# Scaled V in three bfloat16 parts for the neighbour product, and moved turns and constants, in a four-layer graph network

## The chip, the cores and the metric

The kernel runs on one core of one Trainium2 chip. The metric is the device time of one execution in microseconds (us); lower is better. The core has a matrix engine (PE), a vector engine (DVE), a scalar engine (ACT), a general engine (POOL) and a queue for transfers (SP). Each engine works through its own queue strictly in order; semaphores make one wait for another.

## The reference

There are 512 nodes with 512 features and 16,384 edges (src, dst), and four residual blocks on x, each fed with h = max(layernorm(x), 0): a graph convolution, a four-layer sparse attention with a conditioned norm, a diffusion, and a two-layer relational network with gates. The change is mostly about the third block's adjacency, prepared early:

```python
adj = zeros(N, N); adj[row, col] = 1; adj[col, row] = 1; adj = adj + eye(N)
adj = adj / maximum(adj.sum(axis=1, keepdims=True), 1.0)
out = w[0] * h
cur = h
for i in range(3):
    cur = adj @ cur
    out = out + w[i + 1] * cur
return relu(out)
```

With A the symmetric 0/1 matrix plus identity and R the diagonal of inverse row sums, the three steps are R A, R A R A and R A R A R A. The kernel builds V = A R A and S = w1 A + w2 V + w3 A R V once, so that the whole diffusion later is one product with S, scaled by R.

## The kernel before

The node matrices lie as four chunks (K = 4) of 128 nodes by 512 features. The order of the work on every engine is that of the Python text: the kernel schedules by hand, and no planner moves anything. A product of a 128x128 block with 128x512 f32 values is one call in the text and two PE instructions of 0.43 us; a bfloat16 call is one instruction of 0.22 us. Two PSUM buffers ("ps") serve most products, four ("sp") others, two ("tr") the turns, which is what this text calls the transposes on PE with a copy out by ACT (`transposed`, L116 to L122).

The stages in order of time: the edges become one-hot matrices and window products that count edges and weights (to about 92 us); degrees and the two graph convolution layers (to about 140); the neighbour stage with the entry into attention (to 186); four attention layers, each with a multilayer perceptron (to about 650); diffusion (to 692); the two relational layers (to the end). All along, DVE mixes 60 basis matrices into the relational weights with 120 operations of 2.3 us (L216, L218), placed by calls of `more(n)`, which do n of them; POOL loads a basis of 1 MB whenever one of three buffers comes free.

Names that matter here, in the neighbour stage (L796 to L939):

- `enter_a` to `enter_d` take chunk c of x through the outer norm (relu of it by ACT, L816) and the inner, conditioned norm on DVE, which gives ys[c]. `norm_T(yT, ys[c], c)` turns ys[c] into yT, and `v_part(c)` multiplies it with wv.
- `v_rows(m)` computes the upper part of block row m of V from adj and three exact bfloat16 parts of R A (q_adj): row m is 512, 384, 256 or 128 columns wide. `mirrored` fills the lower part by turns.
- `radj` is A scaled by R in f32, made by four ACT operations (L885). `s_rows(m)` multiplies radj with V in f32, and `s_start` prepares the other terms of S in D1. S lies in the buffer of adj.
- `log_counts` and `log_end` prepare the logarithms of the edge counts for the attention scores.

In an attention layer the output projection follows the heads: `rows_of(c, heads)` adds the heads' products of chunk c, DVE adds them to z (L1086), `norm_chunk` makes ys[c], `norm_T` turns it, and `m1(half, j)` is the first matrix of the perceptron on half the nodes. One `more` call stands before the projection and one in the perceptron.

In the diffusion and the relational layers `plain_norm(c)` needs two ACT operations (Ln and Exp, L133 and L134), and `plain_T` turns its result.

At the start POOL builds the identity and the ids, issues its fifteen transfers of constants, and then computes `freq` (seven small operations and an iota) and fills `edge_of` and `sizes` (an iota and 36 fills), which are read from about 40 us on.

Of the kernel before, what the change touches and what calls it, by code (L numbers as in the profile page):

```python
# [9 lines left out]
F32 = mybir.dt.float32  # L10
F16 = mybir.dt.float16
BF16 = mybir.dt.bfloat16
I32 = mybir.dt.int32
AF = mybir.ActivationFunctionType
OP = mybir.AluOpType
# [4 lines left out]
P = 128  # L20
N = 512
D = 512
E = 16384
K = N // P
EC = E // P
H = 4
NB = 4
# [28 lines left out]
def row_bcast(v, parts=P):  # L56

    n = 1
    for s in v.shape:
        n *= s  # L60
    return bass.AP(tensor=v.tensor, offset=v.offset, ap=[[0, parts], [1, n]])
# [6 lines left out]
def network(ctx, tc, a, out, flag_i, general):  # L68
# [44 lines left out]
    def nodes(xT, c, w, **kw):  # L113

        return product([(xT[:, k, chunk(c)], w[:, k, :]) for k in range(K)], **kw)
# [113 lines left out]
    def more(n):  # L229
        for _ in range(n):  # L230
            next(terms, None)
# [20 lines left out]
    with ExitStack() as pe:  # L252
# [36 lines left out]
        sel = edges.tile([P, 32], F32, name="sel")  # L289
        nc.gpsimd.tensor_tensor(sel, ident[:, 0:32], ident[:, 32:64], op=OP.add)  # L290
        nc.gpsimd.tensor_tensor(sel, sel, ident[:, 64:96], op=OP.add)
        nc.gpsimd.dma_start(b_gcn, a["L0_gnn_b_gcn"].rearrange("l (k p) -> p l k", p=P))
        for l, r in enumerate((row1, row2)):
            nc.gpsimd.dma_start(r, row_bcast(a["L0_gnn_b_mlp"][l]))
        phase = edges.tile([64, N], F32, name="phase")
        nc.gpsimd.dma_start(phase, row_bcast(a["node_vec1"], 64))
        f_w1 = edges.tile([64, 16], F32, name="f_w1")
        nc.gpsimd.dma_start(f_w1, a["L1_gnn_f_w1"])
        f_w2 = edges.tile([16, 16], F32, name="f_w2")
        nc.gpsimd.dma_start(f_w2, a["L1_gnn_f_w2"])  # L300
        f_b = edges.tile([16, 2], F32, name="f_b")
        nc.gpsimd.dma_start(f_b[:, 0:1], a["L1_gnn_f_b1"].rearrange("(p o) -> p o", o=1))
        nc.gpsimd.dma_start(f_b[:, 1:2], a["L1_gnn_f_b2"].rearrange("(p o) -> p o", o=1))
        for t, n in ((bq, "bq"), (bk, "bk"), (bv, "bv"), (b1, "m_b1")):
            nc.gpsimd.dma_start(t, a["L1_gnn_" + n].rearrange("b (k p) -> p b k", p=P))
        nc.gpsimd.dma_start(dw, row_bcast(a["L2_gnn_diffusion_weights"]))
        nc.gpsimd.dma_start(att[:, 0, :], row_bcast(a["L3_gnn_att1"]))
        nc.gpsimd.dma_start(att[:, 1, :], row_bcast(a["L3_gnn_att2"]))

        freq = edges.tile([64, 4], F32, name="freq")  # L310
        nc.gpsimd.iota(freq[:, 0:1], pattern=[[0, 1]], base=0, channel_multiplier=1,
# [14 lines left out]
        for i, (lo, hi, _, c0, c1) in enumerate(PIECES):  # L326
            nc.gpsimd.memset(edge_of[:, 0, i : i + 1], float(c1))
            nc.gpsimd.memset(edge_of[:, 1, i : i + 1], float(c0))
            if i in (0, 2):
                nc.gpsimd.memset(sizes[:, :, i:], float(hi - lo))  # L330

        def look_for_stray():

# [461 lines left out]
    def norm_T(yT, y, c):  # L795
        transposed(yT[:, :, chunk(c)], [y[:, chunk(k)] for k in range(K)], nc.scalar.copy)  # L796
# [21 lines left out]
    def enter_c(c):  # L818
        mv = moments(z[:, c, :])
        inner[c] = rsqrt_start(mv[:, 1:2], EPS, [P, 1])  # L820
        ys[c] = att_y.tile([P, D], F32, name="y")
        nc.vector.scalar_tensor_tensor(ys[c], z[:, c, :], mv[:, 0:1], mod[:, 0, c, :], op0=OP.subtract, op1=OP.mult)

    def enter_d(c):
        n = rsqrt_end(*inner[c])
        nc.vector.scalar_tensor_tensor(ys[c], ys[c], n, mod[:, 1, c, :], op0=OP.mult, op1=OP.add)

    def v_part(c):
        if general:
            nc.vector.tensor_tensor(v[:, c, :], nodes(yT, c, wv), bv_row, op=OP.add)  # L830
        else:
            nc.scalar.copy(v[:, c, :], nodes(yT, c, wv))
# [3 lines left out]
    V = CP  # L836

    def upper(m, parts):
        ps = sp.tile([P, D], F32, name="sp")
        calls(ps[:, m * P :], [(lhs[:, k, chunk(m)], rhs[:, k, m * P :]) for k in range(K) for lhs, rhs in parts])  # L840
        return ps[:, m * P :]
# [4 lines left out]
    def s_start(m):  # L846
        d = D1[:, m, m * P :]
        nc.vector.tensor_scalar(d, d, dw[:, 1:2], None, op0=OP.mult)
        nc.vector.scalar_tensor_tensor(d, V[:, m, m * P :], dw[:, 2:3], d, op0=OP.mult, op1=OP.add)

    def s_rows(m):
        nc.vector.scalar_tensor_tensor(S[:, m, m * P :], upper(m, [(radj, V)]), dw[:, 3:4], D1[:, m, m * P :],
                                       op0=OP.mult, op1=OP.add)

    def mirrored(res, m):
        if m < K - 1:
            transposed(res[:, m + 1 :, chunk(m)], [res[:, m, chunk(q)] for q in range(m + 1, K)], nc.scalar.copy)

    def log_counts(k):

        nc.vector.tensor_scalar(lnC[:, k, :], C[:, k, :], 1.0, None, op0=OP.max)
        nc.scalar.activation(lnC[:, k, :], lnC[:, k, :], AF.Ln)
        nc.vector.tensor_scalar(C[:, k, :], C[:, k, :], 0.0, NEG, op0=OP.is_equal, op1=OP.mult)
# [17 lines left out]
    v_rows(1)  # L881
    enter_c(0)
    mirrored(V, 0)
    for k in range(K):
        nc.scalar.mul(radj[:, k, :], adj[:, k, :], rinv[:, k : k + 1])  # L885
    enter_c(1)
    enter_d(0)
    enter_a(3)
# [13 lines left out]
    enter_c(2)  # L902
    s_start(2)
    s_start(3)
    S = act.tile([P, K, N], F32, name="adj")
    s_rows(0)
    enter_d(2)
    v_part(1)
    enter_b(3)
    norm_T(yT, ys[2], 2)  # L910
    log_counts(1)
    s_rows(1)
    enter_c(3)
    mirrored(S, 0)
    log_counts(2)
    if not general:
        ps = mm.tile([P, N], F32, name="ps")
        for j in range(3):
            nc.tensor.matmul(ps[:1, :1], n_bad[:, j : j + 1], ones, start=(j == 0), stop=(j == 2))
        nc.vector.tensor_scalar(flag_i, ps[:1, :1], 0.5, None, op0=OP.is_gt)  # L920
    v_part(2)
    enter_d(3)
    s_rows(2)
    norm_T(yT, ys[3], 3)
    mirrored(S, 1)
    s_rows(3)
    log_end(0)
# [10 lines left out]
    with ExitStack() as ph:  # L938
# [61 lines left out]
        for i in range(NB):  # L1000
# [52 lines left out]
            def rows_of(c, heads, ps=None, last=False):  # L1053

                first = ps is None
                if first:
                    ps = mm.tile([P, D], F32, name="ps")
                calls(ps, [(oT[:, j, chunk(c)], wo[:, j, :]) for j in heads], first=first, last=last)
                return ps

            ps_ = [rows_of(0, (0, 1))]
            more(6)
            pT = att_p.tile([P, K, N], F32, name="pT", bufs=2)
            turn(pT, head, (0, 1))
            ps_.append(rows_of(1, (0, 1)))
# [11 lines left out]
            for c in range(K):  # L1077
                if c < 2:
                    ps = rows_of(c, (3, 2), ps_[c], last=True)
                else:  # L1080
                    ps = rows_of(c, (0, 1))
                    if c == 3:
                        norm_T(yT, ys[1], 1)
                        ys.append(norm_chunk(mod, 2))
                    rows_of(c, (2, 3), ps, last=True)
                nc.vector.tensor_tensor(z[:, c, :], ps, z[:, c, :], op=OP.add)  # L1086
                if c == 2:
                    norm_T(yT, ys[0], 0)
                else:
                    ys.append(norm_chunk(mod, c))  # L1090
            tT = one.tile([P, K, N], F32, name="oT")

            def m1(half, j):
                cols = slice(half * 256, half * 256 + 256)
                ps = mm.tile([P, D], F32, name="ps")
                for k in range(K):
                    nc.tensor.matmul(ps[:, :256], w1[:, k, chunk(j)], yT[:, k, cols],  # L1097
                                     start=(k == 0), stop=(k == K - 1))
                nc.scalar.activation(tT[:, j, cols], ps[:, :256], AF.Relu, bias=b1[:, i, j : j + 1])  # L1099

            m1(0, 0)
            norm_T(yT, ys[2], 2)
            m1(0, 1)
            m1(0, 2)
            norm_T(yT, ys[3], 3)
            m1(0, 3)
# [4 lines left out]
            else:  # L1111
# [3 lines left out]
                bo = load_row(a["L1_gnn_bo"][i + 1])  # L1115
                mod = new_mod()
                modulation(mod, 0)
            more(6 if i < NB - 1 else 5)
            for j in range(K):
                m1(1, j)  # L1120
            if i == NB - 1:
# [35 lines left out]
    def plain_norm(c):  # L1157

        y = late.tile([P, D], F32, name="y", bufs=4)
        mv, n = stats(x[:, c, :])  # L1160
        nc.vector.tensor_scalar(y, x[:, c, :], mv[:, 0:1], n, op0=OP.subtract, op1=OP.mult)
        return y

    def plain_T(hT, y, c, copy=relu_neg):
        transposed(hT[:, :, chunk(c)], [y[:, chunk(k)] for k in range(K)], copy)
# [2 lines left out]
    ys = []  # L1168
    for c in range(K):
        nc.vector.tensor_tensor(x[:, c, :], nodes(tT, c, w2), x[:, c, :], op=OP.add)  # L1170
        ys.append(plain_norm(c))
        if c == 2:
            plain_T(hT, ys[0], 0)
    plain_T(hT, ys[1], 1)
    cur = one.tile([P, 2, K, D], F32, name="mod")
    for c in range(K):
        nc.vector.tensor_tensor(cur[:, 0, c, :], nodes(hT, c, w_diff), b_diff, op=OP.add)
# [7 lines left out]
    for c in range(K):  # L1185
        tot = cur[:, 1, c, :]
        nc.vector.scalar_tensor_tensor(tot, nodes(S, c, cur[:, 0, :, :]), rinv[:, c : c + 1], tot,
                                       op0=OP.mult, op1=OP.add)
        nc.vector.scalar_tensor_tensor(x[:, c, :], tot, 0.0, x[:, c, :], op0=OP.max, op1=OP.add)
        ys.append(plain_norm(c))  # L1190
        if c == 2:
            plain_T(hT, ys[0], 0)


    wr = wl1
    for l in range(2):
# [29 lines left out]
            u2 = late.tile([P, R, K, D], BF16, name="u2")  # L1226
            u = [[u01[:, 0, r, :, :], u01[:, 1, r, :, :], u2[:, r, :, :]] for r in range(R)]
        ws = [w.rearrange("p (k o) -> p k o", k=K) for w in wr]
        plain_T(hT, ys[1], 1, turned)
        gates = [gates_start(0)]  # L1230
        for c in range(K):
            ps0, ps1 = (nodes(hT, c, ws[r], pool=sp, name="sp") for r in range(R))
# [87 lines left out]
```

## Time and profile before

| | |
|---|---|
| runs | 825.98, 826.07, 827.73 us; median 826.07 |
| profiled execution | 826.12 us, span 824.3 us |
| PE busy, 140 to 168 us | 26.30 of 28.00 us |
| PE busy, 168 to 186.24 us | 17.92 of 18.24 us; DVE 12.62, ACT 7.53 |
| PE busy, 262 to 385 us (one layer's length) | 122.45 of 123.00 us; DVE 114.42 |
| PE busy, 692 to 819.6 us | 126.80 of 127.60 us; DVE 78.47 |
| first window product on PE (L598) | starts at 9.31 us |
| first q projection of attention on PE | starts at 186.24 us |

A row of a timeline below gives start and length in us, the engine, the source line, the operation, out<-in with shapes, how many alike were merged, and in brackets the idle time before it with what ended it. The list of waits gives, for an engine and a releasing line, the total, the number and the longest.

### The profile page before, as it was taken

The numbers are of one execution on the slowest core, as the hardware profiler recorded it, in microseconds if no ns is written. First come the engines' busy times: TensorE is split into PE (matmuls) and PEld (weight loads), VectorE is DVE, ScalarE is ACT, GpSimd is POOL, SyncE is SP. The second block draws the span as 40 slices with busy tenths as digits, with TensorE's granted clock in tenths as the row PEclk, the third lists the DMA queues.
The fourth block names the chain that finished last, engine by engine and source line by source line (L and its number), as shares of the span: only waits on it lengthen the run. The fifth ranks groups of instructions, "written<-read, shape, count | busy, mean of one in ns | idle before, by whom it ended". The sixth has DMA issues, their size and how long they took to land.

```text
span 824.3 us, 8236 instructions
## 1 busy us (share of the span) xinstructions
PE 805.4 (98%) x2586; PEld 391.3 (47%) x2597; DVE 679.9 (82%) x1199; ACT 326.0 (40%) x657; POOL 64.3 (8%) x135
## 2 busy tenths in 40 slices
PE   7999999999999999999999999999999999999997
PEld 3444344454444744444644445644445644444445
DVE  5977986978889999889997889999889977789530
ACT  5454414534652424662424752324653122310410
POOL 8000010000000101001101000101010100000000
PEclk9999999999999999999999999999999999999999
DMA  9200155305658557587558586655599631122001
GB/s 231 74 7 17 43 215 193 114 2 167 182 164 286 180 184 230 139 247 268 184 162 285 148 259 226 200 161 190 146 297 384 214 92 53 47 84 100 1 13 41
DMA packets 50833, 128.38 MB, mean 156 GB/s; under 512 B 7008, under 2 KB 7808, under 8 KB 49760
## 3 DMA queue, kind: packets, MB, share of 16 engines
q0 software_dynamic: 17552, 66.83, 25.4%
q1 hardware_dynamic: 32944, 60.84, 23.8%
q8 instruction: 22, 0.36, 0.2%
q14 instruction: 27, 0.22, 0.1%
q10 hardware_dynamic: 288, 0.13, 0.1%
HBM read 108.90 MB, written 6.29 MB: 140 GB/s over the span
## 4 chain that ended last, share of the span: by engine, by line
PE 61%; issue 18%; DVE 13%; DMA 4%; ACT 2%; POOL 1%; SPq 0%; DVEq 0%; POOLq 0%
PE ps L101 31%; PE ps L1097 7%; PE sp L101 7%; DVE wrel L218 7%; PE win L598 4%; PE sp L968 4%; PE ps L376 4%; DMA basis<-in_L_gnn_basis_dram 2%; PE tr L121 2%; PE sp L702 1%; DVE st L158 1%; DMA w<-in_L_gnn_root_dram 1%; DMA w<-in_L_gnn_W_mlp_dram 1%; ACT p L974 1%; DVE y L792 1%
## 5 line engine op out<-in xcount | busy, mean ns | idle before, releaser
L218 DVE SCALAR_TENSOR_TENSOR wrel<-basis,att,wrel 128x2048 f32<-128x2048 f32 x116 | 264.8, 2342 | 1.4 <-DMA basis<-in_L_gnn_basis_dram 1.4
L101 PE MATMUL ps<-w,oT 128*128 128x512 f32 (+1 forms) x296 | 130.5, 584 | 1.3 <-DVE z L1086 1.3
L101 PE MATMUL ps<-yT,w 128*128 128x512 f32 x256 | 112.9, 594 | 0.0
L101 PE MATMUL ps<-w,yT 128*128 128x512 f32 x224 | 101.1, 595 | 1.2 <-ACT yT L128 0.7
L202 POOL DMA_DIRECT2D basis<-in_L_gnn_basis_dram x60 | 45.1, 752 | 674.4 <-DVE wrel L218 529.1
L101 PEld LDWEIGHTS ps<-w,oT 128*128 128x128 f32 x296 | 53.9, 190 | 62.7 <-issue 51.4
L101 PEld LDWEIGHTS ps<-yT,w 128*128 128x128 f32 x256 | 48.2, 190 | 61.9 <-issue 60.9
L101 PEld LDWEIGHTS ps<-w,yT 128*128 128x128 f32 x224 | 41.1, 190 | 47.2 <-issue 43.8
L133 ACT ACTIVATE g<-mv,eps_t 128x1 f32<-128x1 f32 (+1 forms) x45 | 13.3, 295 | 117.8 <-DVE mv L160 116.4
L1097 PE MATMUL ps<-yT,w 128*128 128x256 f32 x256 | 58.3, 381 | 0.0
L968 PE MATMUL sp<-kT,qT 128*128 128x512 f32 x128 | 57.5, 592 | 0.0
L972 DVE CUSTOM_DVE_ANT_0 ns<-sp,lnC 128x512 f32<-128x512 f32 x64 | 43.6, 689 | 13.7 <-PE sp L968 13.5
L974 ACT ACTIVATE p<-ns,stat 128x512 f32<-128x512 f32 x64 | 45.6, 713 | 22.9 <-DVE stat L972 22.5
L1097 PEld LDWEIGHTS ps<-yT,w 128*128 128x128 f32 x256 | 47.4, 190 | 10.6 <-ACT oT L1099 3.1
L598 PE MATMUL win<-s_hot,st 128*128 128x512 bf16 x189 | 50.5, 379 | 0.3
L579 DVE TENSOR_SCALAR s_hot<-node_ids,e_c 128x512 bf16<-128x512 f16 x128 | 39.4, 354 | 6.1 <-PE win L598 5.9
L960 ACT ACTIVATE p<-p,stat 128x512 f32<-128x512 f32 x64 | 43.7, 706 | 0.0
L968 PEld LDWEIGHTS sp<-kT,qT 128*128 128x128 f32 x128 | 24.3, 190 | 30.6 <-issue 30.1
L704 ACT ACTIVATE mod<-sp 128x512 f32<-128x512 f32 x64 | 32.9, 599 | 8.6 <-PE sp L702 8.6
L598 PEld LDWEIGHTS <-st 128*128 128x128 bf16 x195 | 18.5, 98 | 37.3 <-issue 24.3
L121 PEld LDWEIGHTS tr<-ident,y 128*128 128x128 f32 x176 | 21.5, 141 | 23.1 <-issue 16.3
L963 DVE STREAM_TRANSPOSE turned<-p 128x512 f32<-128x512 f32 x48 | 31.0, 685 | 1.7 <-issue 0.6
(276 smaller groups left out, 1076.9 us busy)
## 6 DMA issues: line engine op xcount, KB each, us to landing
basis<-in_L_gnn_basis_dram POOLq DMA_DIRECT2D x60, 1024.0 KB, 6.7
pT<-turned SPq DMA_DIRECT2D x192, 64.0 KB
w<-in_L_gnn_m_w_dram SPq DMA_DIRECT2D x8, 1024.0 KB
w<-in_L_gnn_wv_dram SPq DMA_DIRECT2D x4, 1024.0 KB
w<-in_L_gnn_wq_dram SPq DMA_DIRECT2D x4, 1024.0 KB
w<-in_L_gnn_wk_dram SPq DMA_DIRECT2D x4, 1024.0 KB
w<-in_L_gnn_wo_dram SPq DMA_DIRECT2D x4, 1024.0 KB
w1d<-wrel POOLq DMA_DIRECT2D x2, 1024.0 KB, 6.3
```

The source lines that it names most:

```text
L101: nc.tensor.matmul(ps, lhsT, rhs, start=(first and i == 0), stop=(last and i == len(parts) - 1))
L121: nc.tensor.transpose(ps[:, i, :], b, ident)
L202: nc.gpsimd.dma_start(t.rearrange("p (k o) -> p k o", k=K), by_partition(a[f"L3_gnn_basis{l + 1}"][b]))
L218: nc.vector.scalar_tensor_tensor(w, t, s, w, op0=OP.mult, op1=OP.add)
L376: nc.tensor.matmul(bank[0], lhsT, rhs, start=(i == 0), stop=(i == len(parts) - 1))
L579: nc.vector.tensor_scalar(s, node_ids, src[:, c : c + 1], None, op0=OP.is_equal)
L598: nc.tensor.matmul(banks[w], st[:, c - g0, :, :], s, start=(left[w] == total[w]), stop=(left[w] == 1))
L960: nc.scalar.mul(ps_[c], ps_[c], st[:, 2:3])
L968: nc.tensor.matmul(ps, qT[:, chunk(c)], kT, start=True, stop=True)
L972: nc.vector.tensor_tensor_reduce(ns, ps, lnC[:, c, :], -1.0, 3e38, OP.add, OP.min, st[:, 0:1])
L974: nc.scalar.activation(p, ns, AF.Exp, bias=st[:, 0:1], scale=-1.0, accum_out=st[:, 1:2])
L1097: nc.tensor.matmul(ps[:, :256], w1[:, k, chunk(j)], yT[:, k, cols], start=(k == 0), stop=(k == K - 1))
```

## The change

1. `radj` is no longer made. After V is whole, `scaled(k)` makes three bfloat16 parts of R V, row block by row block: ACT writes the leading part, DVE the remainder in place of V, ACT its leading part, DVE the rest. `s_rows` multiplies adj, which is 0 and 1 (and 2) and so exact in bfloat16, with the three parts. S moves to radj's buffer, and RV takes that of q_adj.
2. The rest of the neighbour stage is put in another order: `v_part(1)`, `v_part(2)`, `enter_b(3)`, `enter_c(3)` and `log_counts` come before the first `s_rows`, with the four `scaled` among them.
3. In attention, for chunk 3 one more head's product comes before `norm_T(yT, ys[1], 1)`; `norm_T` of chunk 2 stands behind `m1(0, 1)`; and in layer 0 one basis operation goes from the first `more` to the second.
4. In diffusion, and at its end, `plain_T(ys[c - 2])` stands before `plain_norm(c)`.
5. POOL's `freq`, `edge_of` and `sizes` are computed before the transfers of the constants are issued instead of after.

```diff
@@ POOL at the start @@
         nc.gpsimd.tensor_tensor(sel, sel, ident[:, 64:96], op=OP.add)
+        freq = edges.tile([64, 4], F32, name="freq")
+        nc.gpsimd.iota(freq[:, 0:1], ...)
...
+        for i, (lo, hi, _, c0, c1) in enumerate(PIECES):
+            nc.gpsimd.memset(edge_of[:, 0, i : i + 1], float(c1))
+            nc.gpsimd.memset(edge_of[:, 1, i : i + 1], float(c0))
...
         nc.gpsimd.dma_start(b_gcn, a["L0_gnn_b_gcn"].rearrange("l (k p) -> p l k", p=P))
...
@@ the neighbour stage @@
+    def scaled(k):
+        r = rinv[:, k : k + 1]
+        nc.scalar.mul(RV[:, 0, k, :], V[:, k, :], r)
+        nc.vector.scalar_tensor_tensor(V[:, k, :], V[:, k, :], r, RV[:, 0, k, :], op0=OP.mult, op1=OP.subtract)
+        nc.scalar.copy(RV[:, 1, k, :], V[:, k, :])
+        nc.vector.tensor_tensor(RV[:, 2, k, :], V[:, k, :], RV[:, 1, k, :], op=OP.subtract)
+
     def s_rows(m):
-        nc.vector.scalar_tensor_tensor(S[:, m, m * P :], upper(m, [(radj, V)]), dw[:, 3:4], D1[:, m, m * P :],
-                                       op0=OP.mult, op1=OP.add)
+        nc.vector.scalar_tensor_tensor(S[:, m, m * P :], upper(m, [(adj, RV[:, i, :, :]) for i in range(3)]), dw[:, 3:4],
+                                       D1[:, m, m * P :], op0=OP.mult, op1=OP.add)
...
     mirrored(V, 0)
-    for k in range(K):
-        nc.scalar.mul(radj[:, k, :], adj[:, k, :], rinv[:, k : k + 1])
     enter_c(1)
...
     s_start(3)
-    S = act.tile([P, K, N], F32, name="adj")
-    s_rows(0)
+    S = radj
+    RV = act.tile([P, 3, K, N], BF16, name="C01")
+    scaled(0)
     enter_d(2)
+    scaled(1)
     v_part(1)
     enter_b(3)
     norm_T(yT, ys[2], 2)
+    scaled(2)
+    enter_c(3)
+    scaled(3)
+    v_part(2)
     log_counts(1)
+    log_counts(2)
+    s_rows(0)
+    enter_d(3)
     s_rows(1)
-    enter_c(3)
-    mirrored(S, 0)
-    log_counts(2)
...
-    v_part(2)
-    enter_d(3)
+    mirrored(S, 0)
+    norm_T(yT, ys[3], 3)
     s_rows(2)
-    norm_T(yT, ys[3], 3)
     mirrored(S, 1)
     s_rows(3)
@@ attention @@
-            more(6)
+            more(6 if i else 5)
...
-                    if c == 3:
+                    if c == 2:
+                        rows_of(c, (2, 3), ps, last=True)
+                    else:
+                        rows_of(c, (2,), ps)
                         norm_T(yT, ys[1], 1)
                         ys.append(norm_chunk(mod, 2))
-                    rows_of(c, (2, 3), ps, last=True)
+                        rows_of(c, (3,), ps, last=True)
...
             m1(0, 0)
+            m1(0, 1)
             norm_T(yT, ys[2], 2)
-            m1(0, 1)
             m1(0, 2)
...
-            more(6 if i < NB - 1 else 5)
+            more((7, 6, 6, 5)[i])
@@ diffusion; the same once more in its last loop @@
+        if c > 1:
+            plain_T(hT, ys[c - 2], c - 2)
         ys.append(plain_norm(c))
-        if c == 2:
-            plain_T(hT, ys[0], 0)
-    plain_T(hT, ys[1], 1)
```

More of the change, by code (lines that the diff above doesn't have):

```diff
@@ L291, in network @@
         nc.gpsimd.tensor_tensor(sel, sel, ident[:, 64:96], op=OP.add)
[L292 to L308, printed above, removed]
         freq = edges.tile([64, 4], F32, name="freq")
@@ L330, in network @@
                 nc.gpsimd.memset(sizes[:, :, i:], float(hi - lo))
+        nc.gpsimd.dma_start(b_gcn, a["L0_gnn_b_gcn"].rearrange("l (k p) -> p l k", p=P))
+        for l, r in enumerate((row1, row2)):
+            nc.gpsimd.dma_start(r, row_bcast(a["L0_gnn_b_mlp"][l]))
+        phase = edges.tile([64, N], F32, name="phase")
+        nc.gpsimd.dma_start(phase, row_bcast(a["node_vec1"], 64))
+        f_w1 = edges.tile([64, 16], F32, name="f_w1")
+        nc.gpsimd.dma_start(f_w1, a["L1_gnn_f_w1"])
+        f_w2 = edges.tile([16, 16], F32, name="f_w2")
+        nc.gpsimd.dma_start(f_w2, a["L1_gnn_f_w2"])
+        f_b = edges.tile([16, 2], F32, name="f_b")
+        nc.gpsimd.dma_start(f_b[:, 0:1], a["L1_gnn_f_b1"].rearrange("(p o) -> p o", o=1))
+        nc.gpsimd.dma_start(f_b[:, 1:2], a["L1_gnn_f_b2"].rearrange("(p o) -> p o", o=1))
+        for t, n in ((bq, "bq"), (bk, "bk"), (bv, "bv"), (b1, "m_b1")):
+            nc.gpsimd.dma_start(t, a["L1_gnn_" + n].rearrange("b (k p) -> p b k", p=P))
+        nc.gpsimd.dma_start(dw, row_bcast(a["L2_gnn_diffusion_weights"]))
+        nc.gpsimd.dma_start(att[:, 0, :], row_bcast(a["L3_gnn_att1"]))
+        nc.gpsimd.dma_start(att[:, 1, :], row_bcast(a["L3_gnn_att2"]))
         def look_for_stray():
@@ L1189, in network @@
         nc.vector.scalar_tensor_tensor(x[:, c, :], tot, 0.0, x[:, c, :], op0=OP.max, op1=OP.add)
+        if c > 1:
+            plain_T(hT, ys[c - 2], c - 2)
         ys.append(plain_norm(c))
-        if c == 2:
-            plain_T(hT, ys[0], 0)
     wr = wl1
@@ L1228, in network @@
         ws = [w.rearrange("p (k o) -> p k o", k=K) for w in wr]
-        plain_T(hT, ys[1], 1, turned)
+        if l == 1:
+            plain_T(hT, ys[1], 1, turned)
         gates = [gates_start(0)]
```

## The prediction

> **What bounds the kernel now.** The page first, for the engines' shares.
>
> ```profile
> span 824.3 us, 8236 instructions
> ...
> PE 805.4 (98%) x2586; PEld 391.3 (47%) x2597; DVE 679.9 (82%) x1199; ACT 326.0 (40%) x657; POOL 64.3 (8%) x135
> ...
> PEclk9999999999999999999999999999999999999999
> ```
>
> PE is busy nearly throughout at full granted clock, so a change pays by taking work off PE or by closing PE's waits, and costs where it opens new ones. Second, the list of waits, for PE:
>
> ```profile
> PE tr L121 <- DVE y L792: 2.2, 4, 0.6
> PE ps L101 <- DVE z L1086: 1.3, 1, 1.3
> ...
> PE ps L101 <- ACT yT L128: 0.7, 1, 0.7
> PE ps L376 <- DMA w<-in_L_gnn_W_mlp_dram: 0.7, 1, 0.7
> ...
> PE sp L101 <- ACT yT L128: 0.6, 1, 0.6
> ```
>
> Each is one place that the change touches; all together are 5.5 us. Third, the timeline of the neighbour stage (168 to 186 us), the only one where work is exchanged:
>
> ```profile
> 168.08 0.27 PE L121 MATMUL tr<-ident,CP 128*128 128x128 f32 x1
> 168.19 2.74 PE L101 MATMUL sp<-CP,AT 128*128 128x512 f32 x6
> ...
> 169.35 0.55 DVE L815 TENSOR_SCALAR z<-x,mv,n 128x512 f32<-128x512 f32 x1
> 169.93 0.63 ACT L816 ACTIVATE z<-z 128x512 f32<-128x512 f32 x1 [1.50 <-DVE z L815]
> 170.47 0.57 ACT L122 COPY yT<-tr 128x512 f32<-128x512 f32 x1
> ...
> 172.22 3.60 PE L101 MATMUL ps<-w,yT 128*128 128x512 f32 x8
> ...
> 173.64 0.74 DVE L852 SCALAR_TENSOR_TENSOR adj<-sp,dw,D 128x512 f32<-128x512 f32 x1
> ```
>
> See that PE reaches the first neighbour product (L852's, tile sp) at 168.19, while ACT's copy of the second node chunk, which v_part(1) reads, ends only at 171.04: that product is what fills PE meanwhile. DVE has no idle time from 153 to 169.9, so nothing earlier moves this. Fourth, an existing split into three bfloat16 parts, at L1240 to L1246, is the price list of the new one:
>
> ```profile
> 701.91 0.62 ACT L1245 CAST mod<-rest 128x512 bf16<-128x512 f32 x1 [0.82 <-DVE rest L1244]
> 702.44 0.68 ACT L1240 ACTIVATE mod<-sp,gate 128x512 bf16<-128x512 f32 x1
> 702.56 0.69 DVE L1246 TENSOR_TENSOR u<-rest,mod 128x512 bf16<-128x512 f32 x1 [0.68 <-ACT mod L1245]
> 703.17 0.74 DVE L1244 SCALAR_TENSOR_TENSOR rest<-sp,gate,mod 128x512 f32<-128x512 f32 x1
> ```
>
> A split goes DVE, ACT, DVE in series: 2.04 us from one L1244 to the same place of the next, 0.68 of it DVE waiting.
>
> **The change, part by part.** *Products.* The four f32 products start 176.10 to 178.68 for 384 columns (2.58 us), 182.86 to 184.58 for 256 (1.72), 185.24 to 186.13 for 128 (0.89), and 8 x 0.43 = 3.43 for 512: 8.62. The L844 products have the new form (12 bfloat16 calls each): 147.69 to 150.28, 153.71 to 155.66, and 1.98 for the last two: 6.52. PE work falls by 2.1.
>
> *The chain in their place.* ACT loses four L885 (0.71 each, idle ground on its queue) and gains eight operations; DVE gains eight. In the built queues ACT has the copy of yT for chunk 2 behind both operations of scaled(0) and scaled(1) and behind chunk 3's relu; that relu waits for DVE's L815, behind the splits 0 and 1. Walking on from the rows, with 0.04 from engine to engine:
> - PE: mirrored(V, 2) done 168.2; v_part(1) waits for the copy, 171.1 to 174.5. Wait 2.9.
> - DVE: s_start ends where L852 stood, 173.64. Split 0 to 175.67 (0.74, copy 0.62, 0.69, overlapped as above), enter_d(2) to 176.86, where it was 175.49. PE's transposes of chunk 2: 176.9. Wait 2.4.
> - DVE: split 1 to 178.8, L142 and L147, L815 to 179.8; ACT: relu from 179.85, copy 180.4 to 180.97. v_part(2): 181.0 to 184.5. Wait 3.7 after the transposes.
> - Split 2, whose ACT multiply stands behind that copy: 181.6 to 183.7; enter_c(3) to 185.4; multiply 3 at 185.15, split 3 from 185.9 to 188.0. PE's s_rows(0) starts at 184.5, would end at 187.1 (2.59 long), gets its last part at 188.06 and ends at 188.3. Wait 1.2.
> - s_rows(1) to 190.2; DVE does two pairs of log_counts (0.8 each) and S row 0 to 190.3, y of chunk 3 at 191.4: wait 0.7; s_rows(2), s_rows(3) and the turns end at 194.2.
>
> There q_of(0) starts; before it was 186.24. **Stage: +7.9** (waits of 2.9 + 2.4 + 3.7 + 1.2 + 0.7 = 10.9, less 2.1 of work and 0.9 of waits and starts that PE has there now). Attention's DVE work shifts alike: L218 starts 3.9 behind q_of(0) now and 3.8 in the walk. The one price with no row, L1244 with both operands in SBUF, lies between 0.69 (L1246) and 0.75; I take 0.74, nearest in form. With 0.1 either way for each of some 15 handovers the stage is +6.4 to +9.4.
>
> [...]
>
> *Fillers.* One more f32 call (two instructions of 0.43) stands before norm_T(ys[1]) now. The group of 262.60 ends 264.32, the transposes start 265.03, so 0.71 is lost, in four layers; y then has 0.15 to spare and norm_T(ys[2]) moved behind m1(0, 1) keeps the gain. Cover gone: less than 0.71 back. **-2.8.** *more(5) in layer 0*: the z wait (258.63 against 257.16) goes, -1.5, since L218's sixth call, which waited for its basis until 255.5, follows PE's need. Its 2.3 us move to the second more(), where z at L1127 came 0.2 after PE; it ends 2.0 late relative to PE. PE has 2.6 there, but the nine L218 of the next start (302.42) then leave kT of head 1 late: its slack is 330.93 - 329.47 = 1.46, and 0.3 to 0.9 goes back. I take 0.6: **-0.9**. *plain_T before plain_norm*: copies at 661.52 and 691.59 stood behind the next norm's Ln and Exp; PE was ready at 661.28 and 691.48, started 662.15 and 692.22: **-1.6**.
>
> *Constants.* POOL's 1.6 us of freq and 1.3 of fills go ahead of its transfers, so 0.64 MB of rows and phase leave 3 us later and W_mlp's last chunk may land before PE asks: at most the 0.8 around 13.59. Fifteen transfers move, behind 45 POOL operations. Against the gain, one row:
>
> ```profile
> 18.71 1.48 DVE L579 TENSOR_SCALAR s_hot<-node_ids,e_c 128x512 bf16<-128x512 f16 x1
> ```
>
> Its kind takes 0.34 elsewhere; it lay under the fills (18.74 to 19.95). These fall at about 5.3 to 6.6 now, on the path of vals to the first window product: 0 to +1.1, some of it inside the DMA wait. The transfers' first reader stands at 42 us; the last lands at 25.7 now and some 3 later then. I take **-0.4** (-0.8 to +1.1).
>
> [...]
>
> **Sum**, on the profiled execution's 826.12 (span 824.3, 1.8 around it; median 826.07): +7.9 - 2.8 - 0.9 - 1.6 - 0.4 = +2.2, so **828.3 us**.
>
> **Rivals.**
> 1. *Cheap stage, 0.20.* Handovers at their low end and a covered split: +6.4 instead of +7.9, 826.8. For it: DVE has 5.6 idle us in the old stage (12.62 busy of 18.24). Against: DVE is busy when it matters, until 173.6.
> 2. *Work decides, 0.13, the faster side.* If the two waits that the splits open (2.4 and 3.7) were hidden, because chunk 2's y and copy come ahead of them in effect, the stage is +1.8 and the time 826.1 + 1.8 - 5.7 = 822.2. With stage waits of 8.7 in all instead of 10.9 the change costs nothing, and from there down it gains. Against: the queue order above.
> 3. *DVE keeps the gains, 0.12.* If z0 and y stay late on DVE because the L218 blocks end with PE already now (287.96 against 288.0), the fillers give back 3.5: 831.8.
> 4. *PE slows after the longest wait, 0.10.* At the start the twelve turns of 5.51 to 8.39 took 0.21 us each, later ones 0.11. If v_part(2) ran at such a half rate it would take 1.7 to 3.4 longer, less 1.2 hidden: +0.5 to +2.2, say 829.6. Against: no row inside the kernel shows it.
>
> The change does what it says: its products are in the built queue as 48 bfloat16 calls.
>
> **How the numbers follow.** The forecast holds 0.45. About 0.2% (1.65 us) can be told from no change: faster below 824.4, slower above 827.7. Rival 2 gives most of faster, 0.13; rival 1 and the forecast's low edge give same, 0.24; the rest is slower, 0.63. Leaving out rival 2 and the worst of rival 3, the range is 825.2 to 831.0; the forecast alone is 827.0 to 829.8.
>
> **What would show it.** Right: PE waits for ACT yT of about 2.9 and 3.7 and for DVE y of 2.4 in the stage, q_of(0) 8 us later, and none left for DVE y L792 and ACT yT L128 after it. Wrong: a stage with less than 8 us of PE waits, a wait at the late kT of layer 1 above 1, or a first window product (9.31 now) over 1 us later. An earlier end of the edge stage (109 us) by more than 1 would break the constants' term.

## The result and the profile after

The changed kernel took 832.64 us (median of 4 runs, 831.93 to 833.48), the kernel before 826.21 (4 runs); the ratio is 1.0075, 95% interval 1.0057 to 1.0093. So it is 6.4 us slower where +2.2 was predicted, outside the range (825.2 to 831.0). The profiled execution is that of 833.48 us, the slowest of the four. From the page of the changed kernel, the span, the engines' shares and the granted clock:

```profile
span 831.7 us, 8278 instructions
...
PE 805.6 (97%) x2601; PEld 391.3 (47%) x2613; DVE 686.5 (83%) x1207; ACT 329.8 (40%) x661; POOL 64.0 (8%) x135
...
PEclk9999999989999999999999999999999999999999
```

PE's busy time did not fall (805.4 before), though by the prediction 2.1 us of its work go, and in the ninth slice the clock isn't full any more. The list of PE's waits in the changed kernel (releaser, total, number, longest):

```profile
PE ps L101 <- ACT yT L122: 7.0, 4, 3.4
...
PE ps L1112 <- DVE z L1101: 2.4, 4, 0.7
PE tr L121 <- DVE y L827: 2.2, 1, 2.2
PE ps L101 <- DVE z L1101: 1.5, 1, 1.5
```

The waits that the change was predicted to close (L792 and L128 of before) are gone. In their place stand the neighbour stage's, and two that the prediction has not: four of up to 0.7 (2.4 in all) at L1112, the perceptron's first matrix, and one of 1.5 for z in layer 2. PE's timeline in the stage:

```profile
170.77 3.70 PE L101 MATMUL ps<-w,yT 128*128 128x512 f32 x8 [2.74 <-ACT yT L122]
176.70 0.63 PE L121 MATMUL tr<-ident,y 128*128 128x128 f32 x4 [2.23 <-DVE y L827]
180.69 6.38 PE L101 MATMUL ps<-w,yT 128*128 128x512 f32 x8 [3.36 <-ACT yT L122]
187.12 4.49 PE L101 MATMUL sp<-C,adj 128*128 128x512 bf16 x23
...
194.90 5.32 PE L101 MATMUL ps<-yT,w 128*128 128x512 f32 x12
```

The three waits are those of the walk (2.9, 2.4 and 3.7 predicted), and q_of(0) starts at 194.90 where it was 186.24. But v_part(2) took 6.38 us, where v_part(1), the same eight instructions, took 3.70. Why is in the table of stretches of the same kernel (length, then busy time and number for PE, PEld, DVE, ACT, POOL; then the granted clock, DMA share, GB/s):

```profile
176.00:179.30 3.30, 0.63 (x4) 0.42 (x4) 2.54 (x6) 1.10 (x2) 0.00 (x0) 1.00 0.03 5
179.30:186.10 6.80, 5.41 (x7) 2.32 (x8) 3.80 (x8) 3.54 (x7) 0.00 (x0) 0.50 0.00 1
```

The granted clock was 1.00 up to 179.30 and 0.50 from there to 186.10.

For the rest of the document the span is cut at points that every kernel has: the first turns of y in the stage (chunk 0), the first product of q and k in each attention layer, and the first relational product. *Stage* is from the first of these to layer 0; *layer 3* holds the diffusion. The numbers are starts of PE instructions in the traces, in us, one profiled execution each; the medians are of all runs, with the ratio to the kernel before in the same session.

```
                     first turns  stage  layer 0     1       2       3   median  ratio (95%)
before                    162.81  33.73   124.09  121.56  121.54  128.49
changed                   162.47  42.73   122.12  121.77  123.48  126.97  832.64  1.0075 (1.0057-1.0093)
E1 neighbours alone       163.66  41.79   121.56  121.55  121.56  128.85  836.10  1.0114 (1.0094-1.0134)
E2 rest alone             164.17  33.76   122.42  121.76  123.73  126.97  823.67  0.9960 (0.9940-0.9980)
E3 PE kept busy           164.12  41.78   122.11  121.77  121.76  126.98  832.49  1.0060 (1.0039-1.0082)
E4 m1 in other banks      163.98  42.63   122.11  121.41  121.42  126.77  832.16  1.0065 (1.0043-1.0088)
E5 fillers as before      162.83  42.04   122.05  121.56  121.55  126.78  832.70  1.0067 (1.0043-1.0091)
E6 one m1 in other bank   164.16  41.79   122.10  120.80  121.76  126.78  831.10  1.0045 (1.0030-1.0059)
E7 y before splits        164.15  39.53   122.11  121.77  121.76  126.98  831.15  1.0047 (1.0032-1.0062)
E8 rest, one m1           164.30  33.75   122.12  120.80  120.80  126.77  822.61  0.9941 (0.9917-0.9964)
E9 E8, terms even         163.44  33.77   121.23  122.29  120.80  132.31  827.66  1.0014 (0.9995-1.0033)
E10 E9, old constants     163.85  33.76   120.76  121.05  120.81  132.82  828.38  1.0023 (1.0006-1.0039)
E11 constants alone       164.34  33.75   123.49  121.55  121.57  128.51  826.93  1.0003 (0.9990-1.0015)
E12 more(5) alone         163.54  34.83   121.94  121.55  121.55  128.51  825.77  0.9986 (0.9973-0.9999)
```

The relational part, to the start of its last product, is 126.93 with the moved turns and 127.03 without, within 0.01 everywhere. The first turns vary by nearly 2 us (162.47 to 164.34) with no order in it, so differences of a microsecond between medians are read only together with the columns.

### The profile page after: what moved, and what is told of

It reads as the page before. It is cut to its first block, busy times and chain, and to the rows that moved or that the text cites. A ratio compares the mean times of both kernels' runs of the same rounds, so it can differ in the third digit from the quotient of the medians.

```text
span 831.7 us, 8278 instructions
## 1 busy us (share of the span) xinstructions
PE 805.6 (97%) x2601; PEld 391.3 (47%) x2613; DVE 686.5 (83%) x1207; ACT 329.8 (40%) x661; POOL 64.0 (8%) x135
## 4 chain that ended last, share of the span: by engine, by line
PE 69%; DVE 18%; issue 9%; ACT 2%; DMA 2%; POOL 0%; SPq 0%; POOLq 0%; DVEq 0%
PE ps L101 37%; DVE wrel L218 9%; PE sp L101 8%; PE win L599 5%; PE ps L377 5%; PE sp L980 5%; PE ps L1112 5%; PE tr L121 2%; DVE st L158 2%; PE sp L703 1%; DMA basis<-in_L_gnn_basis_dram 1%; DVE y L793 1%; DVE z L1101 1%; PE ps L571 1%; ACT p L986 1%
## 5 line engine op out<-in xcount | busy, mean ns | idle before, releaser
L218 DVE SCALAR_TENSOR_TENSOR wrel<-basis,att,wrel 128x2048 f32<-128x2048 f32 x116 | 264.8, 2344 | 1.6 <-DMA basis<-in_L_gnn_basis_dram 1.6
L101 PE MATMUL ps<-w,yT 128*128 128x512 f32 x224 | 103.9, 608 | 7.0 <-ACT yT L122 7.0
L1112 PE MATMUL ps<-yT,w 128*128 128x256 f32 x256 | 59.4, 383 | 2.4 <-DVE z L1101 2.4
L1112 PEld LDWEIGHTS ps<-yT,w 128*128 128x128 f32 x256 | 47.1, 190 | 14.5 <-DVE z L1101 4.1
```

What stands on the lines that cost most here:

```text
L101: nc.tensor.matmul(ps, lhsT, rhs, start=(first and i == 0), stop=(last and i == len(parts) - 1))
L218: nc.vector.scalar_tensor_tensor(w, t, s, w, op0=OP.mult, op1=OP.add)
```

## The experiments

**E1 and E2: the two halves of the change.** E1 is the kernel before with parts 1 and 2 (neighbour products, order of the stage), E2 the kernel before with parts 3 to 5 (fillers and more, turns, constants).

> The kernel before with parts 1 and 2 of the change alone (the split and the new order of the neighbour stage). Theory A (the loss is the three PE waits of the stage, 2.9, 2.4 and 3.5 lost, plus the half clock that follows them): 826.2 + 9 = 835.2 us, between 833.5 and 836.5, with the granted clock at half for one or two stretches of 3.4 us around 180 us. Theory B (the stage is nearly paid by its smaller products, and the moved turns and the basis operation are what costs): 826 to 828. The original forecast had +7.9 for it: 834.1.

> The kernel before with parts 3, 4 and 5 of the change, and the neighbour stage as before. Theory A: constants -0.4, plain_T before the norm -1.6, one basis operation moved -0.9, the filler and the later turn of chunk 2 nothing, because m1(0, 1) now waits for a PSUM buffer: 823.3 us (822 to 824.5). Theory C (the fillers pay as forecast, 2.8): 820.5. Theory B: 827 or more.

E1 took 836.1 us (832.91 to 836.67), 9.2 over the kernel before in that session (826.9); E2 823.67 (822.65 to 826.88), 3.2 under it. +9.2 - 3.2 = +6.0, near the +6.4 of both together: the halves add up, and each missed in the same direction, the first by 1.3 and the second by 2.5 (-5.7 predicted). The profiled execution of E1 is its fastest and that of E2 its slowest; what the other three of E1, at 836, have more than its profile isn't shown.

Two things come out of the columns. In E1 layer 0 is 2.5 shorter than before, with no edit there: PE's waits of 0.77 for kT and 1.30 for z in that layer are not in its trace. The one for z stood behind a basis that landed 1.44 late; it seems that a stage that ends late lets the transfers catch up, so that part of what more(5) was to gain falls away by itself. This is argued and not shown: the wait for kT is also gone in E2, whose stage is on time, and the one for z is 0.60 in E11, which has the code of before from there on and its stage on time. And layers 1 and 2 of E2 are no shorter than before: the fillers pay nothing.

**E3: PE kept busy.** Products with results that nobody reads, in the three long waits of the changed kernel's stage.

```diff
+    def idle(n):
...
+        ps = sp.tile([P, D], F32, name="sp")
+        for i in range(n):
+            nc.tensor.matmul(ps, adj[:, 0, :P], adj[:, 0, :], start=(i == 0), stop=(i == n - 1))
...
     scaled(1)
+    idle(8)
     v_part(1)
+    idle(6)
...
     scaled(3)
+    idle(12)
     v_part(2)
```

> The changed kernel with 8, 6 and 12 bfloat16 products of 128x512 added in the three waits of the neighbour stage, whose sums nobody reads; they need 1.7, 1.3 and 2.6 us and end before what PE waits for comes. Theory A (about 2.6 us of the result are PE at half clock after the waits): no granted clock of one half, v_part(2) at 3.7 instead of 6.4 us, q_of(0) 2.6 us earlier, 830.0 us (829 to 831). Theory D (the half clock costs nothing, as DVE's split ends late anyway): 832.6, or a little more for the added work.

The clock stays full (mean 0.999 over the execution, 0.996 in the changed kernel) and v_part(2) takes 3.70 again, starting 18.21 us after the first turns as in the changed kernel (18.22). But the stage is only 0.95 shorter, 41.78, since s_rows(0) now waits for the last splits, as its own list of waits shows:

```profile
PE sp L101 <- ACT C L857: 0.4, 1, 0.4
PE sp L101 <- DVE C L858: 0.3, 1, 0.3
```

So of the 2.68 that the half clock adds to v_part(2) some 1.7 lie over work that is late anyway. The time, 832.49, is that of theory D; the stage lies between the two theories. The stage without the half clock is +8.05, against +7.9 predicted.

**E4 and E6: the wait of the perceptron's second product.** The timeline of the changed kernel in layer 1 shows where the fillers' gain went:

```profile
394.72 1.97 PE L1112 MATMUL ps<-yT,w 128*128 128x256 f32 x8
...
396.65 0.68 DVE L1101 TENSOR_TENSOR z<-ps,z 128x512 f32<-128x512 f32 x1
...
397.39 1.99 PE L1112 MATMUL ps<-yT,w 128*128 128x256 f32 x8 [0.70 <-DVE z L1101]
```

m1(0, 1) writes to one of the two buffers "ps". m1(0, 0) has the other, and this one holds chunk 3 of the projection until DVE has added it to z (L1101), at 397.33; that add stands behind the norm of chunk 2. E4 puts the four products of the first half in the pool "sp", E6 only the second.

```diff
-                ps = mm.tile([P, D], F32, name="ps")
+                ps = sp.tile([P, D], F32, name="sp") if not half else mm.tile([P, D], F32, name="ps")  # E4
+                ps = sp.tile([P, D], F32, name="sp") if (half, j) == (0, 1) else mm.tile([P, D], F32, name="ps")  # E6
```

> The changed kernel with the first half of the perceptron's first matrix in the pool of four PSUM buffers instead of the pool of two. Theory A (m1(0, 1) waits 0.7 us in each layer for the buffer that DVE's add of chunk 3 to z frees, so the filler's gain is lost): these four waits go, 832.6 - 2.8 = 829.8 us (829 to 831). Theory E (the turn of chunk 2 or 3 waits for DVE's y instead, which is late by as much): 832.6, and the wait appears at the turns.

> The changed kernel with one product of each layer, the second of the first half (m1(0, 1), the one that waits for DVE z), in a buffer of the pool sp; the other three of that half stay where they are, so that the four row-packed products of the modulation should find their buffers free. Nothing is left out. Theory A (the missed wait for the buffer, and it alone, ate the gain of the fillers): no PE wait for DVE z at this product, period of layer 1 from 121.77 to 121.1 or less, in all 2.8 us off: about 829.8. Theory B (DVE keeps the gains, the prediction's third rival: what is won at the fillers is lost at the next place where PE needs DVE): the wait goes, others of 0.5 to 0.7 per layer come, period 121.6 to 121.8, time 832 to 832.6.

In both the four waits are gone, but layer 1 falls by 0.36 in E4 and by 0.97 in E6. In E4 the modulation, whose four small products use "sp" too, takes 1.75 us instead of 1.14. PE's timeline of E4, and then E6's:

```profile
404.08 1.75 PE L703 MATMUL sp<-mod_w,condT 18*128 18x512 f32 x8
```

```profile
395.45 1.97 PE L1112 MATMUL ps<-yT,w 128*128 128x256 f32 x8
397.26 1.89 PE L1112 MATMUL sp<-yT,w 128*128 128x256 f32 x8
398.99 0.60 PE L121 MATMUL tr<-ident,y 128*128 128x128 f32 x4
...
403.41 1.14 PE L703 MATMUL sp<-mod_w,condT 18*128 18x512 f32 x8
```

The four products (two instructions each) take 18 rows of the array each, at row 0, 32, 64 or 96 by the kernel's `tile_position`. In the changed kernel, where they also took 1.14 us, the first starts at 403.65 and all four are at work by 403.68. In E4 the buffer of the fourth is still being read by ACT's L1114, which starts at 404.19 and ends at 404.66. The 0.61 between 1.75 and 1.14 is the difference of the two layers. In E6's layer 1 PE runs without a gap, and theory A holds there. It doesn't hold for the whole, which came to 831.1 and not 829.8. A basis in layer 2 landed 0.87 late, but the columns show more: against the old fillers (E5, next) one free buffer gains 0.76 in layer 1, and nothing in layer 0 (122.10 against 122.05) or layer 3 (126.78 in both). E8, below, has the same two layers without a gain. Its list of PE's waits says where the time went:

```profile
PE ps L101 <- ACT yT L122: 1.5, 2, 1.1
...
PE ps L101 <- DVE x L1174: 0.5, 1, 0.5
```

The 1.1 is at the end of layer 0, where DVE's add to z stands behind the seven L218 of the second more(); the 0.5 is at the diffusion's first add in layer 3, behind five L218. In these two layers it is theory B, the prediction's third rival: PE comes early and waits for DVE.

**E5: the fillers undone.** The changed kernel with the old fillers and the old place of norm_T(ys[2]).

> The changed kernel with the fillers of the out-projection (the last calls of node chunks 2 and 3) and the order of the first half's products put back as they were; nothing is left out. Theory A (the fillers move PE's wait instead of removing it: the 0.7 at the turns of y goes, and 0.7 comes at the second product of the first half, which needs the accumulation buffer that DVE's z add of chunk 3 frees): the waits for DVE z at the second product vanish, four waits for DVE y of about 0.6 come back, the period of layer 1 falls from 121.77 us to about 121.55 and the time is 831.5 to 832.6, no slower than the changed kernel. Theory B (the prediction's: the fillers are worth 2.8): the period of layer 1 rises to about 122.4 and the time to 835.4.

832.7 us (830.76 to 833.97), which the spread can't tell from the changed kernel's, with a layer 1 of 121.56, 0.21 less than in the changed kernel. PE's waits for y of 0.55 are back in layers 1 to 3; layer 0 has none with more(5), with or without the fillers (E12). Theory A by the columns: the fillers moved the wait and lost 0.2 with it in each of layers 1 to 3, and 0.1 in layer 0 (against E3, which has no late basis).

**E7: the stage in another order.** The same operations (in the code below, calls of several lines are joined by semicolons); the turns of chunk 1 ahead of enter_b(2), y of chunks 2 and 3 ahead of most splits, each split in two halves with other DVE work between.

```diff
-    enter_b(2)
     norm_T(yT, ys[1], 1)
     mirrored(V, 2)
+    enter_b(2)
     enter_c(2)
...
+    split_mul(0); v_part(1); enter_d(2); norm_T(yT, ys[2], 2)
+    split_a(0); enter_b(3); split_mul(1); split_b(0); s_start(2); s_start(3); split_a(1); v_part(2)
+    enter_c(3); split_mul(2); split_b(1); split_a(2); split_mul(3); enter_d(3)
+    split_b(2); norm_T(yT, ys[3], 3); split_a(3); log_counts(1); split_b(3); s_rows(0)
```

> The changed kernel with the same operations of the neighbour stage in another order: the turns of the second node chunk ahead of the relu of the third, y of chunks 2 and 3 ahead of most splits, and each split's last DVE operation issued after the next piece of other DVE work, so that DVE needn't wait for ACT. Nothing is left out. Stage from the first turns of y to the first product of q and k: 33.73 us in the kernel before, 42.73 in the changed one. Theory A (the stage is set by DVE's work: eight more operations of about 0.72, 5.8 us, against 5.6 idle before, and the order adds the rest): the waits for yT of 2.7 and 3.4 and for y of 2.2 fall below 1.2 each, one wait for the last splits of 3 to 5 takes their place, stage about 38.5, time about 828.4. Theory B (the order alone made the waits, as the prediction's second rival has it, and the work can be hidden): stage 34.5 or less, time 824.4 or less. Theory C (the stage is a chain that no order shortens): stage above 41.5, time above 831.4.

The stage is 39.53, 3.2 shorter, and the time 831.15 (828.82 to 832.28). PE's timeline and some rows of DVE's in E7:

```profile
170.32 3.70 PE L101 MATMUL ps<-w,yT 128*128 128x512 f32 x8 [0.62 <-ACT yT L122]
174.97 0.63 PE L121 MATMUL tr<-ident,y 128*128 128x128 f32 x4 [0.95 <-DVE y L827]
176.27 3.70 PE L101 MATMUL ps<-w,yT 128*128 128x512 f32 x8 [0.68 <-ACT yT L122]
183.80 1.08 PE L121 MATMUL tr<-ident,y 128*128 128x128 f32 x4 [3.83 <-DVE y L827]
```

```profile
181.08 0.68 DVE L861 TENSOR_TENSOR C<-CP,C 128x512 bf16<-128x512 f32 x1
181.79 0.75 DVE L856 SCALAR_TENSOR_TENSOR CP<-CP,rinv,C 128x512 f32<-128x512 f32 x1
182.46 0.21 DVE L142 SCALAR_TENSOR_TENSOR v<-v,g 128x1 f32<-128x1 f32 x1
182.71 0.16 DVE L147 SCALAR_TENSOR_TENSOR n<-v,g 128x1 f32<-128x1 f32 x1
182.91 0.75 DVE L827 SCALAR_TENSOR_TENSOR y<-y,n,mod 128x512 f32<-128x512 f32 x1
```

The three waits shrink to 0.62 to 0.95, and one of 3.83 for y of chunk 3 takes their place, at a time when DVE runs without a gap. So the order was worth about 3. Rival 2's two waits are nearly gone, and the stage is still +5.8 where that rival had +1.8. DVE's eight operations of about 0.72 come to the same 5.8, which is theory A's account, but this is argued: no run takes them away, and up to some 1.2 of the 5.8 is slower PE work after the 3.83, with a mean granted clock of 0.998 over the execution (1.08 for the turns instead of 0.63; s_rows(0) and s_rows(1) after them 5.42, in E1 4.70). The stage is 1.0 over theory A's 38.5; the time missed its 828.4, and with a spread of 3.5 us it shows less than the column does. Neither of the two orders tried makes the bfloat16 products pay: they save PE about 2 (in E1 they take 6.6 for the 8.6 of before).

**E8, E9, E10: the parts that pay.** E8 is E2 with E6's one buffer. E9 has six terms in each second more() besides; E10 is E9 with the constants where they were.

```diff
-            more((7, 6, 6, 5)[i])
+            more(6)
```

> The kernel before with all parts of the change but the neighbour products, and with m1(0, 1) of each layer in a buffer of the pool sp. Nothing is left out. Without the last of these the same kernel took 823.67 us. Theory A (the fillers pay once the buffer is free): 2.8 less, 820.9, faster than the kernel before by about 5. Theory B (DVE keeps the gains): 823.2 to 823.9.

> The kernel before with all parts of the change but the neighbour products, m1(0, 1) in a buffer of the pool sp, and the second more() of a layer 6 terms in each of the four instead of 7, 6, 6, 5. Nothing is left out. With 7, 6, 6, 5 it took 822.61 us, with a PE wait for yT of 1.1 at the end of layer 0, where the z add of DVE stands behind the seventh term. Theory A (a term too many there makes that wait): the wait goes, the period of layer 0 falls from 122.12 to about 120.9, the time to 821.4. Theory B (the term only changes its place, and the last layer pays): the period of layer 0 falls, that of layer 3 with the diffusion rises by as much, 822.6.

> The kernel of the run above with the transfers of the constants where they stood before. Nothing is left out. Theory A (the prediction's term for the constants, -0.4): 0.4 slower than the run above, first turns of y in the stage no earlier. Theory B (moving them costs time at the start: in seven profiles with them moved five have the first turns of y at 164.0 to 164.3 us, where the profile of before has 162.8): about 1 us faster than the run above.

E8 took 822.61 us (820.77 to 822.93), 3.8 under the kernel before in its session and 10.0 under the changed one; its layers 1 and 2 are 120.80, 0.75 less than those of before. The median is 1.06 under E2's and not 2.8, between the two theories: E2's runs spread over 4 us, and the profiled one has the late basis in layer 2 that E8 has not. The columns say A for layer 1 (121.76 to 120.80), and for layer 2 apart from the basis; in layers 0 and 3 only 0.3 and 0.2 come off (122.42 to 122.12, 126.97 to 126.77), since DVE's waits named above take the rest.

E9 shows theory B, and more of it. Without the seventh term layer 0 falls by 0.9 (in E10 by 1.4), which shows that the term made the wait there; but layer 3 rises by 5.5. DVE's timeline in E9, then PE's:

```profile
640.76 13.66 DVE L218 SCALAR_TENSOR_TENSOR wrel<-basis,att,wrel 128x2048 f32<-128x2048 f32 x6
654.33 0.69 DVE L1174 TENSOR_TENSOR x<-ps,x 128x512 f32<-128x512 f32 x1
```

```profile
655.08 5.40 PE L101 MATMUL ps<-w,oT 128*128 128x512 f32 x8 [2.76 <-DVE x L1174]
```

The sixth term stands in front of the diffusion's first add; PE waits 2.76 instead of 0.50 in E8, the granted clock is 0.55 over 655.00 to 658.50 (the eight instructions take 5.40 instead of 3.70), and the basis of the sixth term before the projection lands 1.3 late. E10 is 0.7 slower than E9, within the spread of either (6 to 8 us), and decides nothing about the constants.

**E11 and E12: two small parts alone.**

> The kernel before with the transfers of the constants moved, and nothing else. Theory A (the prediction's -0.4, bounds -0.8 to +1.1): 825.7 where the kernel before has 826.1. Theory B (they cost about 1 at the start): 827.2. Theory C (the start varies from run to run whatever the order): no difference that the interval shows.

> The kernel before with five terms instead of six in the first more() of layer 0 and 7, 6, 6, 5 in the second, and nothing else. Theory A (the prediction's -0.9: the wait for z of 1.3 in layer 0 goes, 0.6 comes back at the end of that layer): 825.2 where the kernel before has 826.1. Theory B (the move also makes a basis late for layer 2, as the profiles of two kernels with it show, where PE then waits 1.5 to 1.7): the period of layer 2 rises from 121.54 to about 123, and the time is 826 to 827. Theory C (there is nothing to gain, the late transfer only falls elsewhere): period of layer 0 stays at 124.

The constants: 826.93 against 826.75, ratio 0.9990 to 1.0015, theory C. The moved term: 825.77, 0.98 less (0.1 to 2.2 by the interval); layer 0 is 121.94 where E11 has 123.49, 0.66 of wait for yT comes back at its end (298.72), and layer 2 stays at 121.55. Theory A; in this profile the move doesn't make layer 2's basis late. The profile can't give the size alone, since its stage is 1.08 longer than E11's: the granted clock was 0.53 over 165.20 to 168.70, and v_part(0) took 5.40 us instead of 3.70. E2 has the move with a stage on time, and no wait for z at this place either.

## Why the prediction was wrong

By the columns, the changed kernel's profile less that of before. The predicted row has 0.7 for the fillers in each layer, more(5) in layer 0 and plain_T in layer 3.

```
            first turns  stage  layer 0     1     2     3    sum
predicted          -0.4   +7.9     -1.6  -0.7  -0.7  -2.3   +2.2
profiles           -0.3   +9.0     -2.0  +0.2  +1.9  -1.5   +7.3
```

- **The stage: right, and in part by luck.** +7.9 predicted, +8.05 with the clock full (E3, mean 0.999; E1, with a mean of 0.995 and v_part(2) at 5.16 us, has the same), with the waits in the predicted places: 2.74, 2.23 and 3.36 for 2.9, 2.4 and 3.7, and in E3 0.8 and 0.4 for 1.2 and 0.7. They come to 9.6 and not 10.9, and 1.5 and not 3.0 has to be taken off for the +8.05: two errors of about 1.4 that cancel. That the stage is cheap (rival 1) or the order hides the waits (rival 2) fell; E7 shows that another order recovers 3.
- **The half clock: wrong choice.** The prediction's sum has nothing for it, since no row inside the kernel of before shows PE slower. In the changed kernel, after 3.30 us with 0.63 us of PE work in them, the clock was 0.50 for 6.80 us, and v_part(2) took 2.68 longer. This is rival 4, whose 1.7 to 3.4 was the author's estimate. The price for the stage, 0.95 by E3 and nothing in E1, is at the lower end of that rival's +0.5 to +2.2 or below it, since s_rows(0)'s wait covers most of it.
- **The fillers, -2.8: the step that failed.** The wait for y is closed as predicted, but "y then has 0.15 to spare and norm_T(ys[2]) moved behind m1(0, 1) keeps the gain" is wrong: that m1 needs the buffer which DVE's z add of chunk 3 frees, and in the new order PE comes to it 0.70 early (0.37 in layer 0). The fillers cost 0.2 in each of layers 1 to 3 and 0.1 in layer 0 (E5 against E3): +0.7 in place of -2.8, a miss of 3.5 where the whole is 4.2 in medians; the other misses below and above it add to that, and layer 0's recovered waits take off. The buffer is not all. With it free the fillers gain 0.76 against the old ones in each of layers 1 and 2 (E6, E8: 120.80), 1.5 of the 2.8. In layer 0 more(5) alone had already closed the wait for y (E12), and PE waits 1.07 for yT at the layer's end; in layer 3 it waits 0.50 for DVE's add to x. Both stand behind blocks of L218, so rival 3, DVE keeping the gains, is what happens in these two layers once the buffer is free.
- **more(5), -0.9: right alone (-0.98, E12), wrong in the sum.** Its wait is of layer 0, and with a stage that ends 8 late that layer's waits for kT and z are gone without it (E1: 121.56). On top of the late stage the move costs 0.5 (E5's layer 0 is 122.05). The two terms were added as if independent.
- **plain_T, -1.6: right.** Layer 3 falls from 128.51 (E11) to 126.78 (E5), -1.7.
- **Constants, -0.4: not shown.** Bounds of -0.8 to +1.2 from E11's ratio; zero fits as well.
- **A late basis in layer 2: missed and open.** In the changed kernel's profile PE waits 1.50 for z there, behind an L218 that waits 1.64 for its basis: it makes 123.48 of 121.77. E2 and E6 have it too (1.88 and 0.87 late), E9 in layers 1 and 3, E10 in layer 3; E3, E4, E5, E7 and E8 have not, with nearly the same instructions. What decides it was not found, and how much of the spread between runs of one kernel (1.5 to 8 us) it makes isn't shown.

In medians, E1 says +9.2 for the first half and E2 -3.2 for the second, against +7.9 and -5.7. The second half's shortfall is the fillers for the most part. The first's 1.3 stays open: in E1's profiled execution (832.91) the half clock did not lengthen the stage (41.79, in E3 41.78) and layer 0 is 2.5 shorter, but the other three are 3.0 to 3.8 us slower, at the same mean clock (0.994 to 0.996), and no profile shows why.

## What to carry to other kernels

When PE's work is reordered around a wait, list for each moved product everything it needs: its inputs, and the buffer that it writes to, with who reads that last. Gains in different places add only if the one doesn't move the time at which the other's wait is decided: here more(5) and the fillers were both to remove layer 0's waits. A stage that trades PE work for DVE work can be paid in DVE's time where DVE has little free; here both orders tried lost by it. A wait that is closed in front of a long block of DVE work can come back behind it. A pool shared with products that run packed is not free even when it has room most of the time.

## What the hardware showed

*Half clock.* In the changed kernel the granted clock was 0.50 from 179.30 to 186.10, after 3.30 us with 0.63 us of PE work in them, and v_part(2) took 6.38 us instead of 3.70. In E9 it was 0.55 over 655.00 to 658.50, after 4.00 us with 1.32 us of PE work in them, and eight f32 instructions took 5.40 us where E8 has 3.70. In E3, where products with unread results left waits of at most 1.01 in the stage, v_part(2) took 3.70. But it was lower without a long wait too: in E12 PE was busy for 3.50 of the 5.20 us before 165.20, none of the waits there was above 1.3, and v_part(0), which starts at 164.84, took 5.40 us. The clock over 165.20 to 168.70 was 0.53:

```profile
165.20:168.70 3.50, 3.50 (x5) 1.29 (x4) 3.33 (x10) 0.85 (x3) 0.00 (x0) 0.53 0.10 35
```

In E5 v_part(0) took 5.40 as well. In the changed kernel, E3 and E6 to E11, behind the same waits of about 1.24 and 0.46, it took 3.70. What decides between the two isn't shown.

The price for the stage varies: with the same operations in the same order it took 41.79 us in E1 and E6, 42.04 in E5, 42.63 in E4 and 42.73 in the changed kernel, at mean clocks of 0.992 to 0.996 over the execution, and in E3 41.78 at 0.999.

*Packed products.* Four products on 18 rows each took 1.14 us together (the changed kernel, E6), and 1.75 when one had to wait 0.61 for its buffer (E4).
